# Moving a sort's buffers to other addresses, and a mixture's last scatters into the scan that follows

## The chip, the cores and the metric

The kernel runs on one core of one Trainium2 chip. A core has five engines that each run their own instruction queue in order: TensorE (PE, matrix products into PSUM), VectorE (DVE), ScalarE (ACT), GpSimd (POOL) and SyncE (SP, which here issues most DMA transfers). Engines wait for each other through semaphores only, so an instruction that waits holds back everything behind it in its own queue. The metric is the device time of one execution in microseconds. Before the change it is 2263.52 us, the median of 18 executions between 2254.49 and 2268.52.

## What is computed

Four layers in a row over x of shape (4, 1024, 128), float32. Each layer has a mixing part and a feed-forward part, and each part ends in a residual sum and a layer norm. The change touches the end of the third layer and the start of the fourth:

```
x = layernorm(x + cosformer_attention(x))        # layer 3, 16 heads of 64
x = layernorm(x + mixture_top2_of_8(x))          # layer 3, each token to two experts
x = layernorm(x + state_space_block(x))          # layer 4, 256 channels x 16 states
x = layernorm(x + mixture_top_p_of_8(x))         # layer 4, dense over all 8 experts
```

The first mixture picks, for each token, the two likeliest of eight experts, and sums their outputs with normalised weights. The state space block computes for every channel e, state n and time l

```
h[e,n,l] = exp(delta[e,l] * A[e,n]) * h[e,n,l-1] + (delta*x)[e,l] * B[n,l]
y[e,l]   = sum_n h[e,n,l] * C[n,l]
```

where B and C are rows that all channels share. The second mixture runs every token through all eight experts and gates the results.

## The kernel before

**Elements and halves.** The batch has four elements of 1024 tokens, numbered 0 to 3. An element has eight chunks of 128 tokens, and the scan stage works on halves of 512 tokens, two for each element, so eight halves, numbered 0 to 7.

**The third layer.** The attention goes through the elements in order. When an element's attention is done, a generator `l2_dispatch` (line 1321) sorts its tokens by expert: the router's probabilities, each token's rank among the experts, counts, prefix sums and destinations, many short DVE operations on tiles of the pool `moed` (`md`). Then it issues 16 indirect DMAs on POOL, the scatters of line 1410, two for each chunk, which write the tokens to a sorted buffer `xrows` in DRAM. Another generator, `l2_ffn` (line 1428), walks through the tiles of all four elements' sorted tokens, 23 tiles of 128 for each element: it loads the rows (`xg`, line 1469), loads the expert's weights (`wx`, line 1485), runs the expert and writes the results to `yrows` (line 1539). When an element's tiles are through, `l2_combine` (line 1545) gathers the results back with 16 indirect DMAs on POOL, the gathers of line 1556 into the single-buffered tile `yg`, in two groups of eight. ScalarE and VectorE then weigh and sum them.

A scatter of elements 0 to 2 also waits for the latest `self.beat`, an instruction on ScalarE of the attention (line 1078); this spreads the scatters out in time. Those of element 3 don't have such a wait.

**The fourth layer's scan.** `l3` (line 1626) goes through the eight halves, and in each through the 16 states (a step of the loop is one state). `l3_scan` does for each state: load the B and C rows, broadcast to all partitions (`bn`, `cn`, line 1871, on SP); the B product on POOL (`db`, line 1876); two scans on DVE (line 1881, with the decay that ScalarE makes in line 1880); the C product on POOL (`hc`, line 1892). The C products are summed over the states by PE, as matmuls with the identity (`pys`); for elements 1 to 3 pairs of them are added first by an accumulating DMA that POOL issues (line 1897). Each step of the loop also takes a step of the next half's preparation, of the rest of element 3's dispatch (`rest`, its scatters), of the first mixture (`moe`), and three or four steps of the second mixture's experts (`work`), which follow the finished halves. The first half is prepared inside the attention stage. Before a half of a new element begins to be prepared, the loop drives `moe` on until this element's combine is done.

**What sets the order.** A scheduler orders the instructions of each engine by its own timing model, within the dependencies; loop steps with higher priority (scan, sum, preparation) go first. SBUF is handed out from stacked pools: a pool that is opened in the place of a closed one waits for the last use of the memory that it covers. The attention's weights are in the pool `w2`; `moed` is opened after it, next to it in the stack. The scan stage's pools (`ssm`, `ssm2`, line 1708) are opened when both are closed, in the same memory. In bytes of each partition, `moed` lies from 150,336 to 159,744, and `ssm2` reaches to 156,288, so that the loads of the first `bn` and `cn` tiles wait for the sort's last use of `moed`, line 1404 for element 3.

Of the kernel before, what the change touches and what calls it, by code (L numbers as in the profile page):

```python
# [71 lines left out]
class Net:  # L72
# [1248 lines left out]
    def l2_dispatch(self, b):  # L1321


        nc, m2 = self.nc, self.m2
        wp, st = m2["md"], m2["st"][b]
        rows = st["rows"]
        pj = lambda s, n: self.psb("pj", s, n)
        pr, g, rank, _, _ = self.router(wp, b, self.wmr, ps=pj)
        yield
        sel = wp.tile([P, NC, NE], F32, name="sel2")  # L1330
        nc.vector.tensor_single_scalar(sel, rank, 2.0, ALU.is_le)
        selm = sel.rearrange("p c e -> p (c e)")
        yield

        pp = pj([P, 2, NC * NE], "ppos")
        self.mm(pp[:, 0], m2["stri"], selm)
        self.mm(pp[:, 1], self.ones, selm)
        cnt = wp.tile([P, 2, NC, NE], F32, name="cnt")
        nc.vector.tensor_copy(cnt.rearrange("p i c e -> p i (c e)"), pp)
        before, tot = cnt[:, 0], cnt[:, 1]  # L1340
        yield
        inc = self.prefix(wp, tot, NC, "inc")

        cmp = wp.tile([P, NE, NC], F32, name="cmp")
        nc.vector.tensor_tensor(
            cmp,
            inc[:, NC - 1, :, None].to_broadcast([P, NE, NC]),
            m2["jn"].to_broadcast([P, NE, NC]),
            ALU.is_gt,
        )  # L1350
        nt = wp.tile([P, NE, 1], F32, name="nt")
        nc.vector.reduce_sum(nt[:, :, 0], cmp, AX.X)
        end = self.prefix(wp, nt, NE, "tend")
        base = wp.tile([P, NE], F32, name="base")
        nc.vector.tensor_sub(base, end[:, :, 0], nt[:, :, 0])
        yield

        off = wp.tile([P, NC, NE], F32, name="off")
        nc.vector.tensor_sub(off, inc, tot)
        nc.vector.scalar_tensor_tensor(  # L1360
            off,
            base[:, None, :].to_broadcast([P, NC, NE]),
            float(P),
            off,
            ALU.mult,
            ALU.add,
        )
        nc.vector.tensor_add(off, before, off)

        cmt = wp.tile([P, NT2, NE], F32, name="cmt")  # L1370
        nc.vector.tensor_tensor(
            cmt,
            end.rearrange("p e o -> p o e").to_broadcast([P, NT2, NE]),
            m2["jt"].to_broadcast([P, NT2, NE]),
            ALU.is_le,
        )
        et = wp.tile([P, NT2], F32, name="et")
        nc.vector.reduce_sum(et, cmt, AX.X)
        st["eti"] = m2["keep"].tile([P, NT2], I32, name="eti", bufs=4)
        nc.vector.tensor_scalar(et, et, NE - 1.0, float(WF2), ALU.min, ALU.mult)  # L1380
        nc.vector.tensor_copy(st["eti"], et)
        yield

        sm = wp.tile([P, NC], F32, name="sm2")
        st["dest"], st["wts"] = [], []
        for k in range(2):
            s = wp.tile([P, NC, NE], F32, name=f"ch{k}")
            nc.vector.tensor_single_scalar(s, rank, k + 1.0, ALU.is_equal)  # L1388
            m = wp.tile([P, NC, NE], F32, name="chm")
            nc.vector.tensor_mul(m, s, off)  # L1390
            d = wp.tile([P, NC], F32, name="chd")
            nc.vector.reduce_sum(d, m, AX.X)
            di = m2["keep"].tile([P, NC], I32, name=f"di{k}", bufs=4)
            nc.vector.tensor_copy(di, d)
            st["dest"].append(di)
            nc.vector.tensor_mul(s, s, pr)
            v = m2["keep"].tile([P, NC], F32, name=f"wt{k}", bufs=4)
            nc.vector.reduce_sum(v, s, AX.X)
            st["wts"].append(v)
            yield  # L1400
        nc.vector.scalar_tensor_tensor(sm, st["wts"][0], 1e-6, st["wts"][1], ALU.add, ALU.add)
        nc.vector.reciprocal(sm, sm)
        for v in st["wts"]:
            nc.vector.tensor_mul(v, v, sm)

        key, put = f"put{b}", []
        yield "put"
        for c in range(NC):
            for k in range(2):
                i = nc.gpsimd.indirect_dma_start(  # L1410
                    out=rows[:, :],
                    out_offset=bass.IndirectOffsetOnAxis(
                        ap=st["dest"][k][:, c : c + 1], axis=0
                    ),
                    in_=self.xN[b][:, c, :],
                    in_offset=None,
                ).ins
                if put:
                    self.tc.declare_no_dep(i, group=key, reason="different rows")
                self.tc.add_to_no_dep_group(key, i)  # L1420
                if b < B - 1:

                    self.tc.add_manual_dep(i, self.beat.name, SYNC, reason="spread out")
                put.append(i)
                yield
        st["put"] = put
        st["out"] = m2["dp"].tile([NT2 * P, D], F32, name="yrows")

    def l2_ffn(self, wp):

        units = [
            dict(st=st, j=j, n=min(4, NT2 - j // 4 * 4))
            for st in self.m2["st"]
            for j in range(NT2)
        ]
        n = len(units)
        side = []
        for t in range(-8, n + 4):  # L1440
            while t + 8 < n and "put" not in units[max(t + 8, 0)]["st"]:
                for g in side[:]:
                    if next(g, self) is self:
                        side.remove(g)
                yield
            if 0 <= t + 8 < n and units[t + 8]["j"] % 4 == 0:
                self.l2_load_rows(units[t + 8], units, t + 8, wp)
            if 0 <= t + 4 < n:
                self.l2_weights(units[t + 4], wp)
            if 0 <= t + 2 < n:  # L1450
                self.l2_load_tile(units[t + 2], units, t + 2, wp)
            if 0 <= t < n:
                self.l2_hidden(units[t], wp)
            if 0 <= t - 2 < n:
                u = units[t - 2]
                self.l2_expert_out(u, units, t - 2, wp)
                if u["j"] == NT2 - 1:
                    side.append(self.l2_combine(u["st"], wp))
            for g in side * 2:
                if next(g, self) is self and g in side:  # L1460
                    side.remove(g)
            yield
        for g in side:
            yield from g
# [81 lines left out]
    def l2_combine(self, st, wp):  # L1546
# [4 lines left out]
        def gather(h, c):  # L1551
            if c == 0:
                yg[h] = wp.tile([P, 2, 4, D], F32, name="yg", bufs=1)
            for k in range(2):
                i = 4 * h + c
                nc.gpsimd.indirect_dma_start(  # L1556
                    out=yg[h][:, k, c, :],
                    out_offset=None,
                    in_=st["out"][:, :],
                    in_offset=bass.IndirectOffsetOnAxis(  # L1560
                        ap=st["dest"][k][:, i : i + 1], axis=0
                    ),
                )

        for h in range(2):
            for c in range(4):
                gather(h, c)
# [54 lines left out]
    def l3(self, moe, fp):  # L1622
# [13 lines left out]
        for i, u in enumerate(halves):  # L1636
            nxt = iter(())
            if i + 1 < len(halves):
                if halves[i + 1]["h"] == 0:
                    while "done" not in self.m2["st"][halves[i + 1]["b"]]:  # L1640
                        next(moe)
                nxt = self.l3_prepare(halves[i + 1])
            u["final"] = i + 1 == len(halves)
            scan = self.l3_scan(u)
            for n in range(NST):
                with self.tc.high_priority(offset=1000):
                    next(scan)
                    next(end, None)
                    next(nxt, None)
                for k in range(1):  # L1650
                    next(self.m2["rest"], None)
                next(moe, None)
                if i == 0:
# [192 lines left out]
    def l3_scan(self, u):  # L1846
# [19 lines left out]
        for n in range(NST):  # L1866
# [22 lines left out]
            if h == 0:  # L1889
                nc.scalar.copy(carry[:, :, n : n + 1], db[:, :, 511:512])  # L1890
            hc = wp.tile([P, 2, 512], F32, name="hc", bufs=4)
            nc.gpsimd.tensor_mul(hc, db, bc[1])  # L1892
            if n in (9, 12):
                self.l3_gate(u, n // 12)
            if n % 2 and b > 0 and not (u["final"] and n == NST - 1):
# [302 lines left out]
def program(tc, io):  # L2198
    with ExitStack() as ctx:
# [9 lines left out]
        with ExitStack() as ff:  # L2209
# [2 lines left out]
            first = ctx.enter_context(tc.tile_pool(name="first", bufs=1, side="right"))  # L2212
            mt = ctx.enter_context(tc.tile_pool(name="moet", bufs=2, side="right"))
            w2 = ExitStack()
            n.l2_attn_load(w2.enter_context(tc.tile_pool(name="w2", bufs=1, side="right")))
            weave(*last)
        wd.close()
# [4 lines left out]

        moe = n.l2_ffn(mt)
        with w2:
            md = w2.enter_context(tc.tile_pool(name="moed", bufs=1, side="right"))
            n.l2_attn(load, n.l2_dispatch, moe, first)
        n.l3_pools(ctx)
        fp = ctx.enter_context(tc.tile_pool(name="top", bufs=2, side="right"))
# [18 lines left out]
```

## Time and profile before

The profiled execution took 2253.29 us, with a span of 2251.5 us on the engines and a mean granted TensorE clock of 0.939.

| what | us |
|---|---|
| median of 18 executions | 2263.52 |
| profiled execution (span) | 2253.29 (2251.5) |
| busy PE, DVE, ACT, POOL | 1976.8, 1361.7, 1183.0, 1023.8 |
| attention's last norm ends (element 3) | 1316.6 |
| sort of element 3 ends | 1342.6 |
| first B product on POOL | 1361.4 |
| first C product of halves 1, 2 and 3 | 1457.1, 1555.3, 1651.7 |
| last C product starts | 2112.4 |

Rows of the profile read: start, duration, engine, line of the kernel, operation, output and inputs by the program's names, shapes, how many in a row, and in brackets how long the engine stood idle before, and what it waited for last. The table of slices gives busy shares in tenths. Windows give, for a stretch of time, its length, then busy us and instruction counts of each engine, the mean granted TensorE clock, the share of time that the DMA engines were busy, and GB/s.

### The profile page before, as it was taken

The numbers are of one execution on the slowest core, as the hardware profiler recorded it, in microseconds if no ns is written. First come the engines' busy times: TensorE is split into PE (matmuls) and PEld (weight loads), VectorE is DVE, ScalarE is ACT, GpSimd is POOL, SyncE is SP. The second block draws the span as 40 slices with busy tenths as digits, with TensorE's granted clock in tenths as the row PEclk, the third lists the DMA queues.
The fourth block names the chain that finished last, engine by engine and source line by source line (L and its number), as shares of the span: only waits on it lengthen the run. The fifth ranks groups of instructions, "written<-read, shape, count | busy, mean of one in ns | idle before, by whom it ended". The sixth has DMA issues, their size and how long they took to land.

```text
span 2251.5 us, 46328 instructions
## 1 busy us (share of the span) xinstructions
PE 1976.8 (88%) x17791; PEld 1384.4 (61%) x17791; DVE 1361.7 (60%) x3705; ACT 1183.0 (53%) x2578; POOL 1023.8 (45%) x813
## 2 busy tenths in 40 slices
PE   6779889899999999999979876689888999898988
PEld 3565565544577777787767663356565656565666
DVE  7767644433455654654555556686878688786522
ACT  6532434312344444444555556476868786777443
POOL 5110411000123244234143329989888989889400
PEclk9778979889999999999999987799999999999999
DMA  3010110050000010031223057466776677776421
GB/s 107 0 38 10 31 38 1 19 177 0 1 3 2 4 37 23 26 90 38 77 80 87 17 163 221 125 182 201 213 205 181 183 184 192 188 206 172 110 61 52
DMA packets 138604, 211.04 MB, mean 94 GB/s; under 512 B 18644, under 2 KB 75981, under 8 KB 137998
## 3 DMA queue, kind: packets, MB, share of 16 engines
q1 hardware_dynamic: 126238, 173.81, 25.6%
q0 software_dynamic: 12144, 34.26, 7.3%
q8 instruction: 140, 2.29, 0.4%
q14 instruction: 82, 0.67, 0.1%
HBM read 160.22 MB, written 23.16 MB: 81 GB/s over the span
## 4 chain that ended last, share of the span: by engine, by line
PE 44%; DVE 12%; ACT 10%; issue 3%; DMA 2%; POOL 1%; SPq 0%; DVEq 0%; POOLq 0%; ACTq 0%
PE py L140 8%; PE ph L140 7%; PE po L1153 5%; PE pqk L140 5%; PE pa_m L140 5%; DVE db L1881 4%; PE kp_mo L140 3%; PE pr L1223 2%; PE pv L140 2%; PE pys L140 2%; PE pt L144 1%; ACT da L1880 1%; ACT hh L2007 1%; PE kp_mo L144 1%; ACT L177 1%
## 5 line engine op out<-in xcount | busy, mean ns | idle before, releaser
L1086 POOL TENSOR_TENSOR qt<-r_q,sb_c_turn 128x256 f32<-128x256 f32 (+1 forms) x256 | 164.4, 662 | 451.4 <-ACT r_q L1078 447.5
L1892 POOL TENSOR_TENSOR hc<-db,cn 128x1024 f32<-128x1024 f32 x128 | 319.2, 2529 | 58.2 <-PE pys L140 27.1
L140 PEld LDWEIGHTS py<-wh,hh 128*128 128x128 f32 x2048 | 251.7, 193 | 78.6 <-issue 46.6
L1876 POOL TENSOR_TENSOR db<-ud,bn 128x1024 f32<-128x1024 f32 x112 | 293.0, 2678 | 7.6 <-ACT dl L1841 5.1
L140 PE MATMUL ph<-xT,wh 128*128 128x512 f32 x512 | 251.8, 610 | 24.4 <-ACT hh L2007 6.9
L140 PE MATMUL py<-wh,hh 128*128 128x128 f32 x2048 | 259.1, 277 | 11.1 <-ACT hh L2007 4.6
L2007 ACT ACTIVATE hh<-ph,sb_cols 128x512 f32<-128x512 f32 x256 | 170.2, 681 | 115.9 <-PE ph L140 89.6
L1144 DVE TENSOR_TENSOR a<-pa_m,sb_c_near 128x256 f32<-128x256 f32 x256 | 96.7, 420 | 201.3 <-PE pa_m L140 201.3
L1101 ACT ACTIVATE kN<-kp_mo,sb_c_trig 128x128 f32<-128x128 f32 x448 | 129.8, 371 | 130.7 <-PE kp_mo L144 122.6
L1880 ACT ACTIVATE da<-dl,aneg 128x512 f32<-128x512 f32 x224 | 153.6, 690 | 74.5 <-DVE db L1881 73.8
L140 PE MATMUL pys<-hc,sb_c_ident 128*128 128x512 f32 x324 | 157.7, 616 | 22.1 <-POOL hc L1892 18.9
L1881 DVE TENSOR_TENSOR_SCAN db<-da,carry,db 128x512 f32<-128x512 f32 x128 | 157.0, 1266 | 21.5 <-POOL db L1876 11.2
L1881 DVE TENSOR_TENSOR_SCAN db<-da,db 128x512 f32<-128x512 f32 x128 | 149.5, 1207 | 11.5 <-ACT da L1880 6.4
L140 PEld LDWEIGHTS ph<-xT,wh 128*128 128x128 f32 x512 | 88.2, 194 | 104.6 <-issue 49.1
L140 PE MATMUL pqk<-xT,wE 128*128 128x256 f32 x512 | 136.4, 390 | 8.2 <-ACT coT L1220 4.2
L2032 DVE SCALAR_TENSOR_TENSOR h_acc<-py,gt,h_acc 128x128 f32<-128x128 f32 x252 | 70.8, 343 | 119.3 <-PE py L140 119.3
L140 PEld LDWEIGHTS pys<-hc,sb_c_ident 128*128 128x128 f32 x324 | 60.1, 198 | 83.9 <-issue 56.1
L140 PEld LDWEIGHTS pqk<-xT,wE 128*128 128x128 f32 x512 | 88.6, 193 | 21.8 <-DVE cv L1063 8.1
L1220 ACT COPY coT<-pt 128x512 f32<-128x512 f32 x64 | 37.5, 586 | 116.9 <-PE pt L144 116.9
L140 PE MATMUL po<-ht,wD 128*128 128x512 f32 x192 | 92.9, 594 | 0.0
L1153 PE MATMUL po<-cv,a 128*64 128x65 f32 x2048 | 88.4, 228 | 0.0
L1556 POOL DMA_INDIRECT yg<-yrows,di x64 | 61.1, 954 | 57.1 <-DVE ch L1388 36.6
(463 smaller groups left out, 4247.6 us busy)
## 6 DMA issues: line engine op xcount, KB each, us to landing
wx<-in_wF SPq DMA_DIRECT2D x92, 384.0 KB, 3.5
bn<-rows SPq DMA_DIRECT2D x128, 256.0 KB, 4.8
cn<-rows SPq DMA_DIRECT2D x128, 256.0 KB, 4.2
wh<-in_wH SPq DMA_DIRECT2D x64, 512.0 KB, 3.8
hc<-hc POOLq DMA_DIRECT2D x47, 512.0 KB, 6.7
xrows<-zero SPq DMA_DIRECT2D x4, 1472.0 KB, 11.9
xg<-xrows SPq DMA_DIRECT2D x20, 256.0 KB, 3.4
yrows<-ys SPq DMA_DIRECT2D x20, 256.0 KB, 3.3
```

What stands on the lines that cost most here:

```text
L140: return self.nc.tensor.matmul(out=out, lhsT=lhsT, rhs=rhs, start=start, stop=stop)
L1086: nc.gpsimd.tensor_mul(u["qt"][:, m, a:], u["q"][:, a:], c2["turn"][:, m, o + a : o + 2 * P])
L1101: self.nc.scalar.activation(u["kN"][:, c, m, :], pk[:, c, :], AF.Copy, scale=trig[:, k, m : m + 1])
L1144: nc.vector.tensor_mul(u["a"][:, i, :, :], pa[i], self.c2["near"][:, None, :].to_broadcast([P, 2, P]),)
L1153: self.nc.tensor.matmul(out=u["po"][self.HALF[j], i, c, :], lhsT=lhsT, rhs=rhs, start=key not in u["begun"], stop=True, skip_group_check=True,
L1556: nc.gpsimd.indirect_dma_start(out=yg[h][:, k, c, :], out_offset=None, in_=st["out"][:, :], in_offset=bass.IndirectOffsetOnAxis(ap=st["des ...
L1876: nc.gpsimd.tensor_mul(db, ud, bc[0])
L1880: nc.scalar.activation(da, dl[:, ec, :], AF.Exp, scale=aneg[:, j : j + 1])
L1881: nc.vector.tensor_tensor_scan(db[:, ec, :], da, db[:, ec, :], carry[:, ec, n : n + 1] if h else 0.0, ALU.mult, ALU.add,)
L1892: nc.gpsimd.tensor_mul(hc, db, bc[1])
L2007: nc.scalar.activation(ht, ph, AF.Relu, bias=self.col("h_b1", i=e * NK + k))
L2032: nc.vector.scalar_tensor_tensor(acc[:, c, :], py[:, c, :], gt[:, c, e : e + 1], acc[:, c, :], ALU.mult, ALU.add,)
```

## The change

The pool `moed` is opened before the attention's weights instead of after them, in the same stack. Its tiles then lie from 180,096 to 189,504, the weights and the attention's tiles move down, and the scan's `bn`, `cn` and `db` tiles lie where the attention's own buffers were: the first of them wait for the attention's last norm. The second mixture's weights (`wh`), which come into memory that `moed` covers now, wait for the sort of element 3.

All scatters, element 3's too, wait for `self.beat`. In the scan stage `self.beat` is now the latest C product. The scatters of element 3 are issued one in each step of the loop, and only from half 1 on.

The gathers of element 1 wait for the latest C product too, and are not issued before the eighth state of half 0 (`c3["late"]`).

The tiles of element 3 go through a pipeline of their own, after that of elements 0 to 2, so that element 2's tiles no longer share it.

```diff
@@ l2_dispatch
-                if b < B - 1:
-
-                    self.tc.add_manual_dep(i, self.beat.name, SYNC, reason="spread out")
+                self.tc.add_manual_dep(i, self.beat.name, SYNC, reason="spread out")
@@ l2_ffn
-
+        yield from self.l2_tiles_of(0, B - 1, wp)
+        yield from self.l2_tiles_of(B - 1, B, wp)
+
+    def l2_tiles_of(self, b0, b1, wp):
 
         units = [
             dict(st=st, j=j, n=min(4, NT2 - j // 4 * 4))
-            for st in self.m2["st"]
+            for st in self.m2["st"][b0:b1]
             for j in range(NT2)
         ]
@@ l2_combine
-                nc.gpsimd.indirect_dma_start(
+                g = nc.gpsimd.indirect_dma_start(
...
-
+                if b == 1:
+                    self.tc.add_manual_dep(g.ins, self.beat.name, SYNC, reason="spread out")
+
+        while b == 1 and "late" not in self.c3:
+            yield
         for h in range(2):
@@ l3
-                        next(moe)
+                        next(moe, None)
...
             for n in range(NST):
+                if n == NST // 2 - 1:
+                    c3["late"] = True
...
-                for k in range(1):
+                if i:
                     next(self.m2["rest"], None)
@@ l3_scan
-            nc.gpsimd.tensor_mul(hc, db, bc[1])
+            self.beat = nc.gpsimd.tensor_mul(hc, db, bc[1]).ins
@@ program
             w2 = ExitStack()
+            md = w2.enter_context(tc.tile_pool(name="moed", bufs=1, side="right"))
             n.l2_attn_load(w2.enter_context(tc.tile_pool(name="w2", bufs=1, side="right")))
...
         with w2:
-            md = w2.enter_context(tc.tile_pool(name="moed", bufs=1, side="right"))
             n.l2_attn(load, n.l2_dispatch, moe, first)
```

In the compiled order POOL's queue then reads, after the attention's last product: B products of states 0 to 2, C product 0, B 3, C 1, C 2, and so on; element 1's two groups of eight gathers stand behind the C product of state 9 and at state 16; element 2's at states 20 and 24 (before: 28 and 32), counted on through the halves; the 16 scatters of element 3 at states 20 to 32; element 3's gathers at 73 and 80 (before: 56 and 62). Element 3's tiles are worked on in states 42 to 72 (before: 20 to 53). ACT has seven table loads fewer. The sets of instructions on the other engines are the same, and their order is the same up to the end of the attention and in the last 140 us.

## The prediction

> **What bounds the kernel now.** I read the page's slices first, then busy time cut at the scan's halves, then GpSimd's (POOL's) timeline at the seam between attention and scan, then what holds up the loads at that seam. The seam, some 1,295 to 1,362 us, and the scan stage after it are all that the change touches.
>
> The page: busy shares in tenths over 40 slices of 56 us.
>
> ```profile
> PE   6779889899999999999979876689888999898988
> POOL 5110411000123244234143329989888989889400
> PEclk9778979889999999999999987799999999999999
> ```
>
> From slice 24 (1,351 us) POOL runs at 8 to 9 tenths until slice 37; TensorE (PE) is almost as full, then alone in the last slices. Windows from each half's first C product to the next's: length, busy us (instructions) of each engine, granted clock, DMA share, GB/s.
>
> ```profile
> core 0: us, PE busy (x) PEld busy (x) DVE busy (x) ACT busy (x) POOL busy (x), PEclk, DMA share, GB/s
> 1381.80:1457.10 75.30, 49.67 (x127) 23.76 (x128) 48.22 (x65) 42.31 (x82) 73.83 (x32) 0.79 0.47 137
> 1457.10:1555.25 98.15, 87.64 (x414) 56.89 (x413) 80.31 (x146) 68.75 (x140) 87.28 (x48) 0.95 0.64 193
> 1555.25:1651.67 96.42, 80.08 (x448) 55.89 (x448) 72.27 (x145) 71.28 (x145) 83.19 (x41) 1.00 0.73 202
> 1651.67:1761.30 109.63, 99.78 (x483) 63.96 (x482) 79.50 (x163) 83.19 (x149) 97.65 (x57) 0.97 0.70 186
> 1761.30:1852.50 91.20, 85.22 (x413) 53.90 (x412) 74.44 (x145) 76.46 (x142) 80.67 (x41) 1.00 0.70 188
> ...
> 2034.20:2112.35 78.15, 74.44 (x379) 50.61 (x380) 55.02 (x102) 46.13 (x73) 68.78 (x35) 0.96 0.67 178
> ```
>
> The first half is POOL's alone (73.8 of 75.3). Later POOL and PE are both near 90% and wait for each other; a half that gets more of either's work gets longer (the fourth, 109.6). The seam, on POOL:
>
> ```profile
> 1294.56 1.41 POOL L1086 TENSOR_TENSOR qt<-r_q,sb_c_turn 128x256 f32<-128x256 f32 x2 [9.49 <-ACT r_q L1078]
> 1332.58 0.99 POOL L1556 DMA_INDIRECT yg<-yrows,di  x1 [36.61 <-DVE ch L1388]
> ...
> 1342.64 0.99 POOL L1410 DMA_INDIRECT xrows<-xN,di  x1 [0.30 <-DVE wt L1404]
> 1343.94 0.98 POOL L1410 DMA_INDIRECT xrows<-xN,di  x1 [0.30 <-issue]
> ...
> 1361.36 2.36 POOL L1876 TENSOR_TENSOR db<-xT,bn 128x1024 f32<-128x1024 f32 x1
> 1363.89 1.00 POOL L1410 DMA_INDIRECT xrows<-xN,di  x1 [0.16 <-issue]
> 1364.92 6.97 POOL L1876 TENSOR_TENSOR db<-xT,bn 128x1024 f32<-128x1024 f32 x3
> ```
>
> POOL stands 36.6 us at the second element's (element 1's) gathers, runs eight of them, then 15 of the last element's (element 3's) 16 scatters, and only then the first B product. The load that this product needs waited too. SP's and VectorE's (DVE's) rows:
>
> ```profile
> 1342.70 0.33 SPq L1871 DMA_DIRECT2D bn<-rows  x1
> ```
>
> ```profile
> 1315.47 1.12 DVE L191 TENSOR_SCALAR xN<-cr,ln_mv,ln_rs 128x128 f32<-128x128 f32 x4
> ```
>
> The load goes out at 1342.70, just after the sort's last operation (the wt multiply of line 1404, 1342.38 + 0.24), since the sorting pool covers the scan's buffers. The attention itself ended at 1315.47 + 1.12 = 1316.6; ud, the product's other operand, was finished at 1295.6.
>
> **The change, part by part.** All sums are against the profiled execution: 2253.3 us (span 2251.5 and 1.8 around it); the median shown is 2263.5, 10.2 above, and I add the same 10.2 to the forecast.
>
> *1. Pool order: the start.* With the sorting pool under the attention's weights' top, the first B load waits for the attention's end alone. It goes out at about 1316.7 and lands 4.8 us later (the page's median for bn): first B product at about 1321.7 instead of 1361.4, **-39.7**. The expert weights' first load (wh) now waits for the sort; experts start only in the second half, so this costs nothing. Bounds: -44.5 (the load lands at once) to -35 (it takes twice the median).
>
> *2. What ran in the gap now runs inside.* POOL's work from first B product to last C product was 256 products at 2.31 (start to start, 2093.48 to 2095.79), 40 gathers at 1.26 (1372.05 to 1380.83 is seven steps of 1.25) and 47 accumulate issues at 0.57: 591 + 50 + 27 = 668 of the 753 us from 1361.4 to 2114.7; 85 were idle. Element 1's first eight gathers and 15 scatters now stand inside this span: 23 x 1.26 = **+29.0**. Nothing hides them: POOL is the first halves' bound. So POOL's balance is -10.7 with equal idle time. Bounds: 23 x 0.95 = 22, if a lone one costs only its busy time, to 23 x (1.26 + 0.16) = 33, with the 0.16 of waiting that the rows above show once more for each.
>
> *3. The sort beside the scan.* Element 3's sort (DVE, 1322 to 1342.6) met an idle or gathering POOL. In the new order it lies between the scans of the first five states. Its rows add to 12.6 us. With ten scans at 1.24 and some 14 tile operations at 0.41, DVE has 31 us to do where POOL has ten products, 23 us, before the fifth state's C product: 8 us of waiting, in a half that has no slack to return it. And 24 of the sort's operations read two SBUF operands. A row of before shows what such an operation meets beside a POOL product:
>
> ```profile
> 773.20 0.95 DVE L1278 TENSOR_TENSOR rt_q<-rt_g,rt_q 128x512 f32<-128x512 f32 x1
> ```
>
> ```profile
> 1328.85 0.68 DVE L1278 TENSOR_TENSOR rt_q<-rt_g,rt_q 128x512 f32<-128x512 f32 x1
> ```
>
> ```profile
> 772.73 0.87 POOL L1086 TENSOR_TENSOR qt<-r_q,sb_c_turn 128x128 f32<-128x128 f32 x2 [5.67 <-ACT r_q L1078]
> ```
>
> 0.95 us under a pair of half-size POOL products, 0.68 alone: +0.27. The scan's products last 2.31 us against the qt group's mean of 0.66; stretched alike, 0.27 x 2.31/0.66 = 0.95 an operation and 24 x 0.95 = 23 us is my estimate of the most; the least is 0, if POOL waits for the scan anyway. I take 6, nearer to the lower end, since a POOL that has run out of scanned states blocks nobody. Part 3: 8 + 6 = **+14**, bounds 0 and +31. A gain is excluded: the sort is pure addition here.
>
> The Trainium skill, "SBUF — State Buffer", section "Who interferes with whom", says that a DVE operation with two SBUF inputs and a POOL operation that reads SBUF take one shared port pair as an exclusive lock, the later one blocking fully. That speaks against this change. By the rule each of the 24 would wait for up to a whole product, 24 x 2.31 = 55 us on DVE at worst and half of that on average; the 0.27 us row agrees in kind, and the row's size is what my sum uses.
>
> *4. Half 1.* Scatters, each tied to a C product, and element 2's 16 gathers make POOL's work of this half 74 + 16 x 1.26 + 16 x 1.26 = 114 us; with element 3's tiles put off, PE has only about 59. POOL's idle time there, 98.15 - 87.28 = 10.9, should shrink, as the waits for PE go: I take 6, **-4** (bounds -11 and 0). PE, left idle, cannot start experts earlier: they need the first half's finished rows. So half 0 is 36 x 2.31 + 16 x 1.26 + 1 idle + 14 = 118 long from 1321.7 (to 1440), half 1 120 (to 1560, against 1555.3).
>
> *5. Halves 2 to 7.* Element 3's tiles come at states 42 to 72 instead of 20 to 53: seven more of them after half 1, at (1.65 + 0.61)/2 + 0.16 = 1.3 us of PE each, +9. Counted by instruction order and mean durations, PE's work by half from the third was 88, 93, 81, 78, 72, 81 and becomes 90, 73, 95, 81, 81, 83; POOL loses element 2's second eight gathers from the third half and gets element 3's in the fifth. Reading times from like rows above (93 of work took 109.6; 81 took 91; 88 took 96.4): about 98, 90, 109, 91, 91, 80 against 96.4, 109.6, 91.2, 90.2, 91.5, 78.2, so 559 against 557: **+2**, bounds -10 (POOL's second-element balance comes back in full) and +9 (all of PE's).
>
> *6. Costed at nothing.* ScalarE (ACT) loses seven table loads, 1.28 us each; it is 65% busy. The new pipeline split removes element 2's wait for element 3's rows; those tiles fill PE in half 0, which POOL bounds. SP's weight loads (wx) stand in one queue with bn and cn and wait for PE to free buffers; in half 0 PE has time. Without that cover a held cn costs POOL some 3 us a time (2.9 was the longest wait for cn before). The stage after the last C product, 2112.4 to 2251.5, keeps its instructions: 0.
>
> Sum without part 6: -39.7 + 29.0 + 14 - 4 + 2 = +1.3; the gather groups at the head of POOL's queue, which now also stand in front of products while their buffer (one yg) waits for the group before to be combined (10.8 to 13.3 us after it in the trace), I put at **+6**, two stalls of 3 us like that for cn; bounds 0 and +15. Together **+7**: profiled 2260.3, median **2270.5**.
>
> **Rivals.**
> *A. Faster: the sort does not hold the scan.* Place: the first five states. If DVE slips the sort between scans and part 3 is 0, the sum is 7 - 14 = -7, 2256; it decides from a part 3 under 2.5. With the gathers not stalling either it is -13 (2250), and with part 5 at -10 as well -25 (2238). For it: POOL's 36.6 us gap is truly gone. Against: DVE's 31 us beside POOL's 23.
> *B. No change.* Part 3 and the stalls come to 9 to 17 together instead of 20: 2259 to 2268. The change then only moves idle time from the seam into the scan.
> *C. Much slower: one long wait chain.* The sort's two-operand rows wait for POOL's products, scans come late, POOL stalls in turn: part 3 at +31, the rest as taken: +24, 2288. It decides from a part 3 of about 25. For it: the 0.95 us row, and the first scans sharing DVE with all the sort.
> *D. Pool order does not do what it says:* a first B load still behind the sort would leave +29 - 4 + 2 and no gain, 2290; only if an overlap with another late tile remains.
>
> **How the numbers follow.** 0.2%, 4.5 us, is about what a measurement of this kernel can tell from no change. My sum's likeliest region, +4.5 to +18, has 0.40; C and D 0.13; B, within 4.5, 0.18; A 0.29. So slower 0.53, same 0.18, faster 0.29. The likeliest case's own range is 2268 to 2282; the range for 8 in 10 cuts A at -17.5 and C and D at +27.5: 2246 to 2291.
>
> **What would show it.** First B product at about 1322; no 36 us wait before element 1's gathers; the sort's L1273 to L1404 rows stretched over more than 25 us, two-operand rows longer than before, and POOL waiting for the scan in states 3 to 6; half 1's first C product at 1434 to 1444, half 2's at 1555 to 1565; a half 1 of about 120 us with PE under 65; half 4 the longest of the later ones; an unchanged 139 us tail. Wrong if half 1 starts by 1428 (the sort costs nothing), or if the later halves lose the lump and sum to under 548.

## The result and the profile after

The changed kernel takes 2302.27 us (median of 10 runs, 2295.91 to 2306.66), the kernel before 2260.81 (62 runs): the ratio is 1.0179, with a 95% interval of 1.0165 to 1.0193, so it is 1.8% or 41 us slower. The forecast was 2270.5 with a range of 2246 to 2291. The direction was right; the size was wrong by a factor of six, and the time lies outside the range.

The page's slices after:

```profile
PE   6789889899899999999888857479898989898998
POOL 5100411000133243234243258899887879778500
PEclk9768989899999999999999969779999999899999
```

A slice is 57.4 us. PE now has a hole at slices 23 to 25 (5, 7 and 4 tenths, 1,320 to 1,490 us), and is nearly full behind it. Windows by half, cut at the first C products as before (length, busy us and instructions of each engine, clock, DMA share, GB/s):

```profile
core 0: us, PE busy (x) PEld busy (x) DVE busy (x) ACT busy (x) POOL busy (x), PEclk, DMA share, GB/s
1331.80:1454.80 123.00, 86.87 (x391) 59.30 (x391) 100.66 (x168) 65.42 (x156) 92.86 (x50) 0.83 0.65 197
1454.80:1569.70 114.90, 73.95 (x249) 38.46 (x250) 74.50 (x140) 68.37 (x126) 105.79 (x65) 0.78 0.34 105
1569.70:1662.30 92.60, 80.03 (x396) 51.97 (x395) 69.57 (x133) 67.16 (x129) 80.72 (x41) 0.94 0.69 185
1662.30:1763.00 100.70, 91.86 (x492) 62.73 (x491) 80.20 (x146) 69.70 (x129) 81.70 (x41) 1.00 0.83 234
1763.00:1880.70 117.70, 102.50 (x534) 68.55 (x534) 81.23 (x169) 82.72 (x164) 96.82 (x57) 1.00 0.65 179
...
1976.00:2082.70 106.70, 94.83 (x426) 59.67 (x424) 75.57 (x149) 68.92 (x119) 81.06 (x41) 0.89 0.62 167
2082.70:2155.30 72.60, 71.10 (x379) 48.38 (x378) 53.13 (x99) 46.70 (x73) 68.59 (x35) 1.00 0.68 177
```

The seam on POOL after:

```profile
1298.99 1.41 POOL L1086 TENSOR_TENSOR qt<-r_q,sb_c_turn 128x256 f32<-128x256 f32 x2 [9.39 <-ACT r_q L1078]
1324.83 7.05 POOL L1883 TENSOR_TENSOR db<-xT,bn 128x1024 f32<-128x1024 f32 x3 [24.43 <-PE ph L140]
...
1350.61 2.35 POOL L1899 TENSOR_TENSOR hc<-db,cn 128x1024 f32<-128x1024 f32 x1 [2.87 <-ACT da L1887]
1352.91 4.74 POOL L1883 TENSOR_TENSOR db<-xT,bn 128x1024 f32<-128x1024 f32 x2
1363.83 2.35 POOL L1899 TENSOR_TENSOR hc<-db,cn 128x1024 f32<-128x1024 f32 x1 [6.18 <-DVE db L1888]
```

The first B product starts 3.9 us after the attention's end (1320.9) instead of 44.8 after it. So the pools did what they were to do. But POOL then stands still in the first states, for the scans on DVE. Those share DVE with the sort, and the sort's rows are these:

```profile
1351.02 1.96 DVE L1316 COPY inc<-cnt 128x8 f32<-128x8 f32 x1
1352.89 0.20 DVE L1317 TENSOR_TENSOR inc<-cnt 128x56 f32<-128x56 f32 x1
1353.13 2.20 DVE L1316 COPY inc<-inc 128x16 f32<-128x16 f32 x1
1355.25 0.20 DVE L1317 TENSOR_TENSOR inc<-inc 128x48 f32<-128x48 f32 x1
1355.37 0.41 DVE L1519 SCALAR_TENSOR_TENSOR sg<-sg,ph 128x256 f32<-128x256 f32 x1
1355.70 1.99 DVE L1316 COPY inc<-inc 128x32 f32<-128x32 f32 x1
```

In the kernel before:

```profile
1334.06 0.17 DVE L1316 COPY inc<-cnt 128x8 f32<-128x8 f32 x1
...
1334.38 0.18 DVE L1316 COPY inc<-inc 128x16 f32<-128x16 f32 x1
```

A copy of 8 numbers a partition takes 1.96 us instead of 0.17. Each long row ends where a POOL product ends: 1351.02 + 1.96 = 1352.98 against 1350.61 + 2.35 = 1352.96. The 45 rows of the sort (lines 1273 to 1404 in the kernel before) add to 11.5 us before and 27.2 after.

Where the 44 us between the two profiled spans (2251.5 and 2295.6) lie, with the distances in us:

| stretch | before | after | difference |
|---|---|---|---|
| up to the attention's end | 1316.6 | 1320.9 | +4.3 |
| attention's end to first B product | 44.8 | 3.9 | -40.9 |
| first B product to half 1's first C product | 95.7 | 130.0 | +34.3 |
| half 1 | 98.2 | 114.9 | +16.7 |
| halves 2 to 4 | 297.2 | 311.0 | +13.8 |
| halves 5 to 7, to the last C product | 259.9 | 274.6 | +14.7 |
| tail | 139.1 | 140.3 | +1.2 |

The 4.3 us stand already at the first product of the third layer's attention (592.0 and 596.3), ahead of anything that the change moves; one kernel below starts this stage at 593.8 in one profile and at 591.6 in another, so I don't count them to the change.

### The profile page after: what moved, and what is told of

Read it like the earlier page. It is cut to its first block, busy times and chain, and to the rows that moved or that the text cites. A ratio compares the mean times of both kernels' runs of the same rounds, so it can differ in the third digit from the quotient of the medians.

```text
span 2295.6 us, 46321 instructions
## 1 busy us (share of the span) xinstructions
PE 1996.1 (87%) x17791; PEld 1394.1 (61%) x17791; DVE 1379.6 (60%) x3705; ACT 1177.5 (51%) x2571; POOL 1025.4 (45%) x813
## 4 chain that ended last, share of the span: by engine, by line
PE 41%; DVE 15%; ACT 11%; issue 3%; DMA 2%; POOL 1%; SPq 0%; DVEq 0%; ACTq 0%; POOLq 0%
PE ph L140 7%; PE py L140 7%; DVE db L1888 6%; PE po L1153 5%; PE pqk L140 5%; PE pa_m L140 4%; PE kp_mo L140 3%; PE pv L140 2%; PE pr L1223 2%; PE pys L140 2%; PE pt L144 1%; PE kp_mo L144 1%; ACT da L1887 1%; ACT hh L2014 1%; ACT L177 1%
## 5 line engine op out<-in xcount | busy, mean ns | idle before, releaser
L1883 POOL TENSOR_TENSOR db<-ud,bn 128x1024 f32<-128x1024 f32 x112 | 282.1, 2562 | 26.1 <-DVE ud L1847 25.8
L140 PE MATMUL ph<-xT,wh 128*128 128x512 f32 x512 | 260.8, 623 | 34.1 <-DVE ln_nm L181 9.8
L140 PE MATMUL pys<-hc,sb_c_ident 128*128 128x512 f32 x324 | 161.9, 627 | 32.0 <-POOL hc L1899 28.5
L140 PE MATMUL pa_m<-r_q,r_k 64*64 64x128 f32 x2048 | 86.8, 285 | 0.0
```

Source lines behind the costliest of these rows:

```text
L140: return self.nc.tensor.matmul(out=out, lhsT=lhsT, rhs=rhs, start=start, stop=stop)
L1883: nc.gpsimd.tensor_mul(db, ud, bc[0])
```

## The experiments

The runs were made in two groups, and the kernel before took 2258 to 2261 us in one and 2294 to 2299 in the other; each ratio is against the kernel before on the same chip, and the halves of a profile are compared within a group. The first group holds the first four kernels below and the two runs that end the part on pool order and ScalarE's copies. Some expectations call the two groups the faster and the slower chip.

**The pool order alone.** Only the two lines that open `moed` are moved.

```diff
             w2 = ExitStack()
+            md = w2.enter_context(tc.tile_pool(name="moed", bufs=1, side="right"))
             n.l2_attn_load(...)
...
         with w2:
-            md = w2.enter_context(tc.tile_pool(name="moed", bufs=1, side="right"))
```

> The kernel before with the pool order alone; scatters, gathers and tiles are issued as before (element 3's tiles at states 21 to 53, first expert at state 31). Theory 1 (two causes: the sort beside the scan costs some 24 us in half 0, and in the changed kernel element 3's late tiles, states 42 to 72, cost PE some 25 more, since PE is 90% busy from the first expert on): first B product at about 1322, -39.7 + 29 for the gathers and scatters now inside + 24 = +13, later halves as before: 2274 (2268 to 2282), the sort again about 40 us long with copies of 2 us. Rival 2 (the sort is the whole loss, lateness costs nothing): near the changed kernel, 2290 to 2302. Rival 3 (the sort costs nothing, only the ties do): -11, about 2250.

2261.24 us, ratio 0.9998 (0.9987 to 1.0010). No expectation met it. Half 0 is 127.6 long from the first B product. POOL's own work in it is 34 products (two B products fewer than in the changed kernel), all 16 gathers of element 1 and 16 scatters: 34 x 2.31 + 32 x 1.26 = 118.9. So POOL waits 8.7 us, against 130.0 - (36 x 2.31 + 16 x 1.26) = 26.7 in the changed kernel. Gathers and scatters without a tie stand where POOL would wait for the sort:

```profile
1351.28 2.34 POOL L1892 TENSOR_TENSOR hc<-db,cn 128x1024 f32<-128x1024 f32 x1 [2.76 <-ACT da L1880]
1353.58 2.40 POOL L1876 TENSOR_TENSOR db<-xT,bn 128x1024 f32<-128x1024 f32 x1
1356.13 0.99 POOL L1556 DMA_INDIRECT yg<-yrows,di  x1 [0.16 <-issue]
```

And while POOL issues gathers, the sort's copies are short again. The third copy of the same prefix sum, which took 1.99 us in the changed kernel:

```profile
1353.80 2.20 DVE L1316 COPY inc<-inc 128x16 f32<-128x16 f32 x1
1355.92 0.20 DVE L1317 TENSOR_TENSOR inc<-inc 128x48 f32<-128x48 f32 x1
1356.04 0.41 DVE L1518 SCALAR_TENSOR_TENSOR sg<-sg,ph 128x256 f32<-128x256 f32 x1
1356.37 0.17 DVE L1316 COPY inc<-inc 128x32 f32<-128x32 f32 x1
```

**All but the pool order.** The same two lines moved back in the changed kernel.

> The changed kernel with the pool order undone; the sort again lies before the scan, while scatters, gathers, split and late tiles (states 42 to 72) stay. First B product right after the sort, at about 1347.5 instead of 1361.4, as no gather or scatter stands before it: -14; 24 indirect transfers inside the scan: +29; no sort cost. Theory 1: late tiles +25 on top, about 2300 (2290 to 2306), half 0 some 105 long, halves 2 to 7 longer than 575 together. Rival 2 (the sort is the whole loss): 2261 + 15 = 2276, halves 2 to 7 near 557. Rival 3 (ties alone): 2300 as theory 1, but with the loss in halves 0 and 1.

2286.27 us, ratio 1.0109 (1.0082 to 1.0136), lower than theory 1 said and higher than its rival. The parts came as expected: first B product 28.5 us after the attention's end, half 0 104.2, halves 2 to 7 581.5. Here the sort runs ahead of the scan, and half 0 has as much POOL work as in the changed kernel (34 products and 20 gathers, 103.7; there 103.3). POOL waits 0.5 us instead of 26.7, so 26 us is what the sort beside the scan costs in the changed kernel. It takes back all of what the earlier start gives (28.5 - 3.9 = 24.6). The wait rows of the changed kernel's half 0 put 12.1 of the 26.7 to the scans by name (total, times, longest); the rest is spread over other releasers:

```profile
POOL hc L1899 <- DVE db L1888: 12.1, 3, 6.2
```

POOL's row with the pool order undone, and the same copy beside an idle POOL:

```profile
1347.93 2.36 POOL L1883 TENSOR_TENSOR db<-xT,bn 128x1024 f32<-128x1024 f32 x1 [49.33 <-DMA bn<-rows]
```

```profile
1336.93 0.17 DVE L1316 COPY inc<-cnt 128x8 f32<-128x8 f32 x1
```

**The split undone.**

```diff
     def l2_ffn(self, wp):
-        yield from self.l2_tiles_of(0, B - 1, wp)
-        yield from self.l2_tiles_of(B - 1, B, wp)
+        yield from self.l2_tiles_of(0, B, wp)
```

> The changed kernel with one pipeline over all four elements' tiles: element 2's last eight tiles and element 3's 23 all run at states 32 to 64 instead of 12 to 17 and 42 to 72. Theory 1 in its form of quantity (what counts is the PE work behind the first expert): eight more tiles there, 8 x 1.3 = +10, 2312. Theory 1 in its form of lateness (what counts is that tiles meet the experts in halves 3 and 4): they end 8 states earlier, -10 to -15, 2288 to 2295. If tiles are hidden anyway: 2302, no change.

2301.38 us, ratio 1.0168 (1.0140 to 1.0196): the changed kernel's time, but not for the reason that the third expectation names. Half 1 is 95.7 instead of 114.9, and halves 2 to 7 are 606.5 instead of 585.6. Element 2's tiles and gathers moved, and what half 1 gained the later halves lost.

**The scatters from half 0 on.**

```diff
-                if i:
-                    next(self.m2["rest"], None)
+                next(self.m2["rest"], None)
```

> The changed kernel with element 3's scatters issued from half 0 on (states 4 to 17 instead of 20 to 32), still tied to C products; element 3's tiles at states 40 to 69 instead of 42 to 72. Where POOL's work sets the halves, 13 scatters x 1.26 = 16 us move from half 1 to half 0: half 0 about 140 to 146, half 1 about 100; the sum is the same, 2302 (2296 to 2308). If the scatters fall into POOL's waits for the sort in half 0 they are free: -12 to -16, 2286 to 2290. Lateness of the tiles, two states: -2 to -4.

2305.25 us, ratio 1.0186 (1.0156 to 1.0216), as where POOL's work sets the halves. Half 0 is 151.8 from the first B product, half 1 is 84.7. Fifteen scatters and eight gathers of element 2 moved into half 0, 35 products and 39 transfers, 130.0 us; POOL's waits there went from 26.7 to 21.8. Of 26.7 us more work, then, only 5 fell into waits. Tied to C products, a scatter stands behind the product that waits too, and here it waits for the sort itself:

```profile
1363.80 0.99 POOL L1410 DMA_INDIRECT xrows<-xN,di  x1 [3.99 <-DVE di L1394]
```

**The split alone**, in the kernel before (second group).

```diff
     def l2_ffn(self, wp):
...
+        yield from self.l2_tiles_of(0, B - 1, wp)
+        yield from self.l2_tiles_of(B - 1, B, wp)
+
+    def l2_tiles_of(self, b0, b1, wp):
...
-            for st in self.m2["st"]
+            for st in self.m2["st"][b0:b1]
...
-                        next(moe)
+                        next(moe, None)
```

> The kernel before with the pipeline split alone. Scatters, gathers of element 1 and the pool stay as before; the split alone moves element 2's last tiles forward (states 9 to 12 instead of 19 to 27) and element 3's back to states 39 to 68 (before: 20 to 53). Theory 1 (late tiles meet the experts and put PE behind): halves 0 and 1 no longer than before, half 4 and half 6 long (115 and 100), halves 2 to 7 together some 575 to 582, 2280 to 2288. Rival 2 (the loss of the changed kernel is in POOL's extra work and the sort, the tiles' place costs nothing): 2257 to 2265. Rival 3 (the split is a gain, as element 2's tiles fill PE's idle time in half 0): 2245 to 2255.

2313.13 us, ratio 1.0057 (1.0037 to 1.0078). Run twice more, beside other kernels:

> The kernel before with the split alone, once more beside the changed kernel. Theory 1 (late tiles are what the change costs beyond the moved transfers): a third to two thirds of the changed kernel's loss over before, 1.006 to 1.012; halves 4 and 6 long as in the changed kernel. Rival 2 (lateness is free): 0.998 to 1.002.

2315.10 us, ratio 1.0083 (1.0059 to 1.0107).

> The split alone. On the faster chip, theory 1 (late tiles cost some 25 us of the changed kernel's 41): 1.008 to 1.012, halves 2 to 7 at 575 to 585 against 557 for before. Rival 2 (lateness is free): 0.998 to 1.002. On the slower chip as already seen, 1.008.

2309.02 us, ratio 1.0048 (1.0028 to 1.0068). So the split alone, which makes element 3's tiles late and element 2's last tiles early, costs 11 to 19 us; rivals 2 and 3 fall, but the 25 us of theory 1 were too many. In the last of these profiles halves 2 to 7 take 580.8, against 562.8 for the kernel before in the same group. Half 0 got 22 us longer (129.8 against 107.8), as element 2's 16 gathers (20 us) went into it, and half 1, which held them, got 21.5 shorter. Half 4 is long, as expected; half 6 is not.

```profile
1507.10:1587.40 80.30, 70.08 (x226) 36.20 (x225) 58.89 (x100) 51.12 (x91) 74.19 (x32) 0.87 0.40 122
...
1788.90:1900.60 111.70, 96.85 (x463) 63.10 (x462) 76.03 (x160) 83.86 (x160) 94.23 (x56) 0.95 0.60 166
```

**The changed kernel, in the second group.**

> The changed kernel itself, beside the three kernels that are compared with it here, since the kernel before took 2261 us on one chip and 2299 on another. On a chip where before takes 2261: 2302, ratio 1.018. On a chip like the slower one, ScalarE's copies having given a ratio of 1.002 there: between 1.002 and 1.018.

2314.85 us, ratio 1.0077 (1.0055 to 1.0098). From the attention's end on its profile repeats the first one: half 0 132.8, half 1 114.9, halves 2 to 7 586.5.

**All but the late tiles**: split and held scatters both undone, pool order and ties kept (the two diffs above together).

> The changed kernel without the split and with the scatters issued from half 0 on: pool order and all ties stay, element 3's tiles are back at states 20 to 53. Each of the two undone alone left the time at 2301 and 2305. Theory 1: either of the two alone holds the tiles back, so undoing both takes the late tiles' cost away; the ties and the sort stay with half 0 some 145 to 150: 2270 to 2282, and halves 2 to 7 below 570. Rival 2 (the ties of scatters and gathers to C products are the loss): 2295 to 2305. Rival 3 (only lateness costs, ties and sort are free as with the pool order alone): 2261.

2307.73 us, ratio 1.0037 (1.0020 to 1.0055).

> The changed kernel with neither split nor scatters held to half 1, once more beside it: pool order and ties stay, element 3's tiles at states 20 to 53. Theory 1: clearly below the changed kernel, by the late tiles' cost of 20 to 25 us; 1.004 to 1.009 of before. Rival 2 (ties are the loss): within 5 us of the changed kernel.

2305.21 us, ratio 1.0030 (1.0018 to 1.0043), beside the changed kernel's 1.0077: 10 us below it, less than theory 1's 20 to 25.

> The changed kernel with neither split nor held scatters, element 3's tiles at states 20 to 53. On the faster chip, theory 1 (late tiles 25, ties and sort the rest): 1.006 to 1.010 against the changed kernel's 1.018. Rival 2 (the ties are the loss, lateness free): 1.016 to 1.020. On the slower chip as already seen, 1.003.

2303.89 us, ratio 1.0041 (1.0027 to 1.0054). The three agree: 7 to 9 us over the kernel before, and some 10 below the changed kernel in this group. But the gain does not lie where theory 1 puts it. Halves 2 to 7 take 588 to 593 us, not below 570, and are no shorter than the changed kernel's 586.5. The gain is in halves 0 and 1, 236 us together against 247.7. Half 0 is 142.4 there, with 119.9 of work, so POOL waits 22.5 us, against 132.8 - 103.3 = 29.5 in the changed kernel here: part of the scatters fell into waits. These runs do not show, then, that the 10 us are the price of the tiles' lateness; both undone parts also move POOL's transfers. A loss in the later halves that goes with late tiles is shown by the split alone.

**The sort's copies and casts on ScalarE**, in the changed kernel.

```diff
-            nc.vector.tensor_copy(u[:, 0:k, :], t[:, 0:k, :])
+            nc.scalar.copy(u[:, 0:k, :], t[:, 0:k, :])
...
-        nc.vector.tensor_copy(st["eti"], et)
+        nc.scalar.copy(st["eti"], et)
...
-            nc.vector.tensor_copy(di, d)
+            nc.scalar.copy(di, d)
```

> The changed kernel with the sort's copies (prefix sums) and casts to int32 issued on ScalarE instead of VectorE; nothing else. In the changed kernel's trace these rows took 0.2 to 2.3 us on VectorE beside POOL's products, 8 us more in all than before, while the two-operand rows took some 6 more. Theory 1 (the sort's rows wait for POOL's products and hold the scan, which holds POOL): half 0, counted from the first B product, 130 becomes 120 to 124, total -5 to -9, 2293 to 2297. Rival (the stretched rows hide beside waits for other things): half 0 at 129 to 131, 2300 to 2304.

2303.12 us, ratio 1.0017 (1.0001 to 1.0032), some 14 us below the changed kernel by the ratios (1.0077), but the expectation's place was wrong: half 0 is 129.4, against 132.8 for the changed kernel in this group and 130.0 in the first. The wait went over to the next row that reads two operands, the adds, 0.2 us each in the changed kernel (two of them in the second row):

```profile
1362.38 1.80 DVE L1317 TENSOR_TENSOR inc<-cnt 128x56 f32<-128x56 f32 x1
...
1364.44 4.33 DVE L1317 TENSOR_TENSOR inc<-inc 128x48 f32<-128x48 f32 x2
```

The largest gain is in half 6, 92.8 instead of 106.7. In the changed kernel POOL stands there for 18.3 us; the waits of POOL in half 6, after and with ScalarE's copies:

```profile
POOL db L1883 <- DVE ud L1847: 18.3, 1, 18.3
```

```profile
POOL db L1883 <- ACT dl L1848: 5.4, 1, 5.4
```

It waits for half 7's preparation, whose transposes come at the tenth state of half 6 (45 us into it) with the change, and at the eighth (34) with ScalarE's copies, as PE's order of experts and preparation came out differently. So this wait hangs on a detail of the schedule, which neither the pools nor the ties mean to touch. It is not worth 14 us to the whole: halves 3 and 7 are 5.8 and 2.0 longer with ScalarE's copies, and halves 2 to 7 together take 581.3 against 586.5; the two profiles differ by 8 us in all.

**Pool order and ScalarE's copies, in the kernel before**: the candidate for a better kernel.

> The kernel before with the pool order, and the sort's copies and casts on ScalarE. With the pool order alone half 0 took 127.6 from the first B product, of which 36 x 2.31 + 32 x 1.26 = 123.5 are POOL's own work. Theory 1: at most 4 us to gain, half 0 at 123.5 to 126, 2256 to 2260; if it is given back in the later halves, where PE is the fuller engine, 2261.

2282.64 us, ratio 0.9913 (0.9882 to 0.9945).

> The pool order alone with the sort's copies and casts on ScalarE, once more, on a chip that runs the changed kernel too. On a chip where before takes 2261, the pool order alone gave 1.000, so 0.996 to 1.000 here, 2253 to 2261; on the slower chip 0.991 again.

2280.13 us, ratio 0.9933 (0.9908 to 0.9957).

> The pool order alone with the sort's copies and casts on ScalarE. On the faster chip, where the pool order alone gave 1.000: 0.996 to 1.000. On the slower one 0.992 again.

2276.29 us, ratio 0.9924 (0.9898 to 0.9951). And both versions in the first group:

> The pool order alone, beside the next kernel. Where before takes 2261: 1.000 again, half 0 some 127.6 from the first B product. Where before takes some 2295: half 0 of before is 12 us longer there (107.8) and that of the kernels with the pool order is not, so 0.991 to 0.995.

2262.39 us, ratio 1.0016 (0.9996 to 1.0036).

> The pool order alone with the sort's copies and casts on ScalarE. If these rows hold up the scan: 2 to 4 us below the pool order alone on the same chip. If POOL's own work of 123.5 us sets half 0: the same as the pool order alone within 2 us, and all of the gain of 0.992 seen on the slower chip is the pool order's.

2256.74 us, ratio 0.9991 (0.9978 to 1.0005), 6 us below the pool order alone. From the attention's end on the two profiles are equal (941.9 us each, half 0 127.7 and 128.4), so this gain is not in the scan; the attention's stage is 6 us shorter (721.0 against 727.1), with the other elements' sorts in it. That the copies do this is not shown: the same version takes 727.5 to 727.8 for that stage in its three profiles of the second group. (Two of the expectations count 36 products in half 0; the traces have 34, which makes POOL's own work 118.9 and not 123.5.) The version is below the changed kernel in both groups, and below the kernel before in the second by 0.7 to 0.9%; in the first the two can't be told apart.

**The kernel before, in the second group.**

> The kernel before itself, for a profile beside the others. On the chip where it takes 2261: as the profile before. On the slower chip (2299): the changed kernel there runs from the attention's end on as on the faster chip, within 3 us, and only starts 13 us later, while the kernel before is 38 longer; so 25 us are lost somewhere between the attention's end and the last C product in this kernel alone. Theory 1: in half 0, where with the split alone POOL waited 8.5 us for the scans: half 0 at 105 to 110 instead of 95.7. Rival: in the seam (first B product more than 46 us after the attention's end). Rival 3: in halves 2 to 7 (over 570).

2296.41 us. Of the 35 us that its profile has over the first one, 12.6 are ahead of the attention's end, 12.1 in half 0 (107.8), as theory 1 said, and most of the rest in halves 1 and 3. Its half 0 has the same instructions as in the first profile, and one new wait for the scans:

```profile
1422.45 6.96 POOL L1892 TENSOR_TENSOR hc<-db,cn 128x1024 f32<-128x1024 f32 x3 [8.51 <-DVE db L1881]
```

The two kernels with the new pool order and the old ties do not have this loss (half 0 is 127.6 to 128.4 long in both groups). From the attention's end on, the kernel before is 22 us longer in the second group's profile than in the first's, the changed kernel only 3. That is 19 of the 25 us by which the change costs less in the second group. What makes the second group slower was not found: products, scans and indirect transfers have the same mean durations within 0.02 us in both. The mean granted clock of the kernel before is 0.930 in this profile and 0.939 in the first.

## Why the prediction was wrong, point by point

- **Part 1, the start: right.** -39.7 forecast, -40.9 measured from the attention's end.
- **Part 2, the transfers inside the scan: right in size.** Half 1 with its scatters and gathers is 114.9 for 114.2 of work; the forecast was 120. POOL's waits went, as part 4 says, and further.
- **Part 3, the sort beside the scan: the right mechanism, mis-sized.** 14 was forecast, with bounds 0 and 31; all but the pool order against all gives 26. I counted 24 rows with two operands and left out copies, casts and compares with one, and these were among the longest (1.96, 2.20, 1.99; a cast 2.32 instead of 0.17). I also took a stretch in proportion to the products' length, 0.95 us a row at most, where each waits to the product's end. The sort's rows grew by 27.2 - 11.5 = 15.7 us; with the 8 us that part 3 has for DVE's own load that makes 24, an estimate, near the 26. The Trainium skill, "SBUF — State Buffer", section "Who interferes with whom", names copy, cast and tensor_scalar among the operations that can take the pair that POOL uses, and says that the second one blocks fully; these rows agree with it.
- **The gathers' stalls, +6: not there.** POOL's longest wait for a gather's buffer was 2.5 us, in half 4.
- **Part 5, halves 2 to 7: the step that failed.** +2 was forecast, with bounds -10 and +9; +28.5 was measured. The six halves took 92.5, 100.8, 117.7, 95.2, 106.8 and 72.6, where 98, 90, 109, 91, 91 and 80 were forecast. Up to half 2's start the sum had held (1560 forecast, 1569.7 measured, 4.3 of it ahead of the change), in part by luck: half 0 was 12 longer and half 1 5 shorter than forecast. I had PE's added work right (+8 when half 2 begins) and read a half's time from a like half's. That leaves out that work moved behind the experts' start is carried on from half to half, and it puts nothing for the clock that PE is granted. From half 2's start to the end, before and after:

```profile
1555.25:2251.50 696.25, 633.06 (x3236) 421.96 (x3235) 462.83 (x949) 468.05 (x827) 495.63 (x252) 0.99 0.60 163
1569.70:2295.50 725.80, 653.08 (x3316) 436.34 (x3314) 467.43 (x953) 463.30 (x827) 492.40 (x251) 0.96 0.60 162
```

PE's busy time grew by 20.0 us, for 8 us of work, and the mean granted clock fell from 0.99 to 0.96. What the clock does to a row, in the changed kernel, first while it was 0.50, then while it was 1.00:

```profile
2229.41 6.54 PE L140 MATMUL ph<-xT,wh 128*128 128x512 f32 x8 [3.67 <-DVE ln_nm L181]
2236.01 3.60 PE L140 MATMUL ph<-xT,wh 128*128 128x512 f32 x8
```

```profile
2229.45:2235.00 5.55, 5.55 (x7) 2.45 (x8) 0.00 (x0) 2.85 (x7) 0.00 (x0) 0.50 0.16 47
2236.05:2239.40 3.35, 3.35 (x10) 1.49 (x9) 0.00 (x0) 2.00 (x3) 0.00 (x0) 1.00 0.00 0
```

The table splits the time that is left when half 2 begins: the matmul work left on PE, each matmul counted at 0.43 us for 512 columns; what PE's busy time lost to a granted clock below 1.00, worked out from the trace's clock records; PE's busy and idle time.

| kernel | PE work left | lost to the clock | PE busy | PE idle | time left |
|---|---|---|---|---|---|
| before (first group) | 591 | 8 | 633 | 63 | 696 |
| before (second group) | 591 | 13 | 638 | 64 | 702 |
| pool order alone | 592 | 15 | 642 | 64 | 706 |
| split alone (third run) | 598 | 17 | 649 | 71 | 720 |
| changed | 599 | 20 | 653 | 73 | 726 |
| all but the pool order | 600 | 23 | 655 | 70 | 725 |
| all but late tiles (third run) | 604 | 18 | 657 | 72 | 729 |
| scatters from half 0 on | 607 | 24 | 666 | 76 | 741 |
| split undone | 609 | 23 | 667 | 83 | 750 |

In every row PE's busy time less its work and less the lost clock is 32 to 35 us. So the changed kernel's 30 us more than before are some 8 of work, 12 of lost clock and 10 of idle PE; with the split undone, 18 us more work go with 15 of clock and 20 of idle time. One piece of POOL's waits is shown, the 18.3 us for half 7's preparation. Why the clock is lower and PE more idle stays open. That the moved work brings them along is argued from the table, not shown by a run that changes it alone, and the pool order alone speaks against work as the only cause: 1 us more of it, 7 more of lost clock.

- **Part 6, the tail: right**, 140.3 against 139.1.
- **Rivals.** C named the sort and its price (+31) rightly but stopped at 2288, as it kept part 5. In the range, nothing stood for a loss in the later halves above 9.
- How the 41 us of the first group split into late tiles and ties was not measured there: the two kernels that come nearest to telling them apart ran in the second group, where the whole is 16, and one of them gains in halves 0 and 1 and not in the later ones.

## What to carry to other kernels

Ahead of moving a stage into the shade of another, list which of its instructions read or write SBUF on DVE while POOL computes, with one operand or two, and price each at the wait to the end of a POOL product, not at its own length. Put POOL's own DMA issues beside such work rather than its products: with the pool order alone the rows that met them stayed short, and POOL waited 8.7 us instead of 26.7. And where a full engine follows, count the work that is still left on it when it fills up, and look at its granted clock: work moved behind that point went here with more than its own time.

## What the runs showed of the hardware

A copy of 128x8 numbers on DVE took 0.17 us beside an idle POOL, one of 128x32 took 0.17 beside POOL's indirect DMA issues, and copies of 128x8 to 128x32 took 1.96 to 2.20 beside POOL products of 2.35 to 2.37. Taking such copies off DVE moved the wait to the next two-operand row (0.20 to 1.80) and shortened half 0 by 3.4 us at most. Eight PE matmuls of 512 columns took 6.54 us at a granted clock of 0.50 and 3.60 at 1.00. PE's granted clock fell to 0.78 in half 1, where it was busy for 74 of 115 us, against 0.95 before.
